# Two-layer adaptive block on one Trainium2 core: layer-0 attention's values and gate turned to have the head dimension on the partitions, with sums of squares as one-column products

## The chip, the core and the metric

The kernel runs on one core of one Trainium2 chip. The metric is device microseconds from launch to end. Three runs of the kernel before gave 1462.98, 1463.49 and 1463.92 us; the median is 1463.49 us. A fourth execution was recorded by the hardware profiler.

The engines are named as in the profile: PE is TensorE's matmul, PEld its weight load, DVE is VectorE, ACT is ScalarE, POOL is GpSimd, SP is SyncE.

## What is computed

The input is 64 sequences of 32 tokens with 256 features, so 2048 tokens. Two layers follow, each with a conditioning step, an attention, a second conditioning step and a feed-forward network. The change touches only layer 0's attention, which for each of 16 heads, with head dimension 128 and 64 slots, computes:

```python
A  = tril(q @ k.T * 128 ** -0.5)          # q, k with rotary embedding
ok = enz * (A @ es)                       # es = exp(s); enz = 1 / cumsum(es)
qv = softmax(ok)
W2 = tril((qv * enz) @ es.T)
o  = W2 @ v                               # v = hs @ Wv.T
g  = hs @ Wg.T
o_n = o * rsqrt(mean(o * o, -1) + 1e-5) * g_norm_weight
out = (o_n * silu(g)) @ Wo.T              # summed over the 16 heads, added to x
```

All arithmetic is float32. Nothing is kept between sequences: the triangle masks are over 32 tokens. In the kernel the softmax's division is left out of `qv`, and the squared sum `rs` goes into the epsilon instead (`e2 = 1e-5 * rs * rs`), since the normalisation that follows removes any factor of a row.

## The kernel before

Layer 0's attention is cut into 32 steps: 4 groups of 4 heads (`hq`) times 8 chunks of 256 tokens (`q`). Each step passes through a dozen stages, and `turn(n)` (line 976) runs stages of four neighbouring steps one after the other, so that each stage's result has time to leave the other engines before the next stage needs it. The order in the source is the order on each engine: nothing is rescheduled, every engine runs its instructions first in, first out. PSUM is one pool of 8 banks; each call of `bank()` takes the bank that was released longest ago, and its first writer waits until the last reader of the bank's former content is done.

A turn's stages in order, with what TensorE does in each (a float32 matmul appears as two matmul records and two weight loads, a transpose as one):

- `slots_exp` (line 748, step n+1): 4 products with 17 rows; ScalarE takes the exponentials.
- `scores` (797, n): 32 products of 64x64 weights and 64 columns; VectorE masks them into `aT`.
- `mix` (878, n-1): 16 products of 64x64 weights and 64 columns, which make W2 transposed; VectorE masks them into `w2T`.
- `leave` (963, n-2): 8 products of 128x128 weights (`ogT`) and 256 columns (`wo`), four accumulated in PSUM for each group of 128 tokens; one VectorE addition of 128x512 puts them on x.
- `project_qk` (693, n+1), first half: 8 products with 256 columns.
- `values` (902, n-1): 16 products, weights `w2T` 64x64, 128 columns of `v`, so that o has tokens on the partitions. The 64x64 weights use a quarter of the array, and the order `quarters` lets four such products run at once. ScalarE then takes 8 times Square of 128x128 with an accumulated sum.
- `attend` (823, n) and `cumsum` (779, n+1): 16 and 8 products on quarters.
- `norm` (927, n-1): VectorE adds `e2`; POOL raises it to the power -0.5, giving `f2` [128 tokens, 8].
- `project_qk`, second half: 8 products with 256 columns.
- `gate` (934, n-1): 8 VectorE instructions of 128x128, o times `f2` (one number for each token) times the gate.
- `weigh` (854, n): POOL multiplies `qv` and `enz` into `qe`; VectorE makes `e2`.
- `project_vg` (725, n), for v and for g: 4 products each with 512 columns (weights are tokens). v is copied by ScalarE; g goes through Silu in 6 instructions of ScalarE.
- `prepare` (199): pieces of the quantisation of later weights, with a few transposes, run at two places of the turn.
- `turn_qe` (867, n): 4 transposes of 128x128, copied by ScalarE.
- `turn_og` (948, n-1): 8 transposes of 128x128, copied by ScalarE in 6 instructions into `ogT`.

After the 32 steps, from about 815 us on, the rest of the kernel works through the same 8 chunks (second conditioning, feed-forward network, layer 1). That part is the same in both kernels. The functions that the change touches, and the turn that calls them:

Of the kernel before, what the change touches and what calls it, by code (L numbers as in the profile page):

```python
# [9 lines left out]
F32 = mybir.dt.float32  # L10
I32 = mybir.dt.int32
AF = mybir.ActivationFunctionType
ALU = mybir.AluOpType
AX = mybir.AxisListType

P = 128
B = 64
T = 32
D = 256
# [56 lines left out]
def mk_kernel(  # L76
# [10 lines left out]
    nc = tc.nc  # L87
    MULT, ADD, SUB, MAX, MIN = ALU.mult, ALU.add, ALU.subtract, ALU.max, ALU.min
# [5 lines left out]
    def bank():  # L94
        return psum.tile([P, 512], F32, tag="ps", name="ps")
# [11 lines left out]
    ident = const("ident")  # L107


    xq = [keep.tile([P, 2, D], F32, tag=f"x{q}", name=f"x{q}") for q in range(8)]  # L110
# [23 lines left out]
    ones = keep.tile([P, P], F32, tag="ones", name="ones")  # L134
    mhalf = keep.tile([P, 8], F32, tag="mhalf", name="mhalf")
# [433 lines left out]
    with ExitStack() as s1:  # L569
        p1 = s1.enter_context(tc.tile_pool(name="p1", bufs=1))  # L570
        work = s1.enter_context(tc.tile_pool(name="work", bufs=2))
# [117 lines left out]
        def at(i):  # L689
            hq, q = steps[i]  # L690
            return hq, q, weights[hq], hsT[q // 2], (q % 2) * 256, state[i]
# [30 lines left out]
        def by_parity(ap):  # L722
            return ap.rearrange("p (r e d) -> p r e d", r=2, e=2)

        def project_vg(i, which):
            hq, q, w, hs, lo, s = at(i)
            wt = w[2 if which == "v" else 3]
            for gi in range(2):
                ps = bank()
                for c in range(2):  # L730
                    nc.tensor.matmul(  # L731
                        ps, lhsT=hs[:, c, lo + gi * P : lo + (gi + 1) * P], rhs=wt[:, c, :],
                        start=(c == 0), stop=(c == 1),
                    )
                t = work.tile([P, 512], F32, tag=which, name=which, bufs=2)
                if which == "v":
                    nc.scalar.copy(t, ps)
                else:
                    to, of = by_parity(t), by_parity(ps)
                    nc.scalar.activation(to[:, :, 0, :], of[:, :, 0, :], AF.Silu)  # L740
                    for half in range(2):
                        here, there = slice(half * 64, half * 64 + 64), slice(64 - half * 64, P - half * 64)
                        nc.scalar.activation(to[here, :, 1, :], of[there, :, 1, :], AF.Silu)
                s[which, gi] = t

        E32 = float(np.exp(np.float32(32.0)))

# [23 lines left out]
        def quarters(product):  # L771


            for e in range(2):
                for at in range(2):
                    out = at ^ e
                    product(e, slice(64 * at, 64 * at + 64), slice(64 * out, 64 * out + 64))
# [76 lines left out]
        def weigh(i):  # L854
            s = state[i]
            qe = work.tile([P, 512], F32, tag="qe", name="qe", bufs=1)
            nc.gpsimd.tensor_tensor(
                qe.rearrange("p (k e m) -> p e k m", k=4, e=2),
                s["qv"].rearrange("p (e k) m -> p e k m", e=2),
                s["enz"].rearrange("p e (k m) -> p e k m", k=4), MULT,  # L860
            )

            e2 = work.tile([P, 8], F32, tag="e2", name="e2")
            nc.vector.scalar_tensor_tensor(e2, s["rs"], 1e-5, s["rs"], MULT, MULT)
            s["qe"], s["e2"] = qe, e2

        def turn_qe(i):
# [32 lines left out]
            s["w2T"] = w2T  # L900

        def values(i):
            s = state[i]
            f = work.tile([P, 8], F32, tag="f", name="f")
            s["f"] = f
            po = [bank(), bank()]
            s["po"] = po
            for k in range(4):
                gi, pr = k // 2, k % 2

                def product(e, rows, out):
                    h = pr * 2 + e
                    nc.tensor.matmul(  # L913
                        po[e][out, k * P : (k + 1) * P], lhsT=s["w2T"][rows, e, k, :],
                        rhs=s["v", gi][rows, h * P : (h + 1) * P], start=True, stop=True,
                    )

                quarters(product)
            for e in range(2):
                for k in range(4):  # L920
                    sq = work.tile([P, P], F32, tag="sq", name="sq", bufs=1)
                    nc.scalar.activation(  # L922
                        sq, po[e][:, k * P : (k + 1) * P], AF.Square,
                        accum_out=f[:, e * 4 + k : e * 4 + k + 1],
                    )

        def norm(i):
            s = state[i]
            nc.vector.scalar_tensor_tensor(s["f"], s["f"], 1.0 / P, s["e2"], MULT, ADD)  # L929
            f2 = work.tile([P, 8], F32, tag="f2", name="f2")  # L930
            nc.gpsimd.tensor_tensor(f2, s["f"], mhalf, ALU.pow)  # L931
            s["f2"] = f2

        def gate(i):

            s = state[i]
            f2 = s["f2"]
            for gi in range(2):
                s["og", gi] = work.tile([P, 4, P], F32, tag="og", name="og")
            for k in range(4):  # L940
                for e in range(2):
                    gi, h = k // 2, k % 2 * 2 + e
                    nc.vector.scalar_tensor_tensor(
                        s["og", gi][:, h, :], s["po"][e][:, k * P : (k + 1) * P],
                        f2[:, e * 4 + k : e * 4 + k + 1], s["g", gi][:, h * P : (h + 1) * P], MULT, MULT,
                    )

        def turn_og(i):
            s = state[i]
            for gi in range(2):  # L950
                ps = bank()
                for h in range(4):
                    nc.tensor.transpose(ps[:, h * P : (h + 1) * P], s["og", gi][:, h, :], ident)  # L953
                t = work.tile([P, 4, P], F32, tag="ogT", name="ogT")
                to = t.rearrange("p (r e) t -> p r e t", e=2)
                of = ps.rearrange("p (r e t) -> p r e t", r=2, e=2)
                nc.scalar.copy(to[:, :, 0, :], of[:, :, 0, :])
                for half in range(2):
                    here, there = slice(half * 64, half * 64 + 64), slice(64 - half * 64, P - half * 64)
                    nc.scalar.copy(to[:, :, 1, here], of[:, :, 1, there])  # L960
                s["ogT", gi] = t

        def leave(i):
            hq, q, w, hs, lo, s = at(i)
            ps = bank()
            for gi in range(2):
                for h in range(4):
                    nc.tensor.matmul(  # L968
                        ps[:, gi * D : (gi + 1) * D], lhsT=s["ogT", gi][:, h, :], rhs=w[4][:, h, :],
                        start=(h == 0), stop=(h == 3),  # L970
                    )
            xf = xq[q].rearrange("p g f -> p (g f)")
            nc.vector.tensor_tensor(xf, ps, xf, ADD)
            s.clear()

        def turn(n):

            def on(i, f, *a):
                if 0 <= i < len(steps):
                    f(i, *a)  # L980

            def more(*at):

                if n in at:
                    next(beyond)

            def ahead():
                if 2 <= n < len(steps):
                    next(preparing, None)

            N = len(steps)
            on(n + 1, slots_exp)
            on(n, scores)
            more(N)
            on(n - 1, mix)
            on(n + 1, slots_clip)
            more(N - 1)
            on(n - 2, leave)
            more(N - 1)
            on(n + 1, project_qk, "q", 0)  # L1000
            on(n + 1, project_qk, "k", 0)
            if n < 2:
                condition(n + 2)
            on(n - 1, values)
            on(n, attend)
            on(n + 1, cumsum)
            more(N)
            on(n - 1, norm)
            on(n + 1, project_qk, "q", 1)
            on(n + 1, project_qk, "k", 1)  # L1010
            on(n - 1, gate)
            on(n, weigh)
            on(n, project_vg, "v")
            on(n, project_vg, "g")
            if n < 2:
                low_rank(n + 2)
            if n < 1:
                gather_cond(n + 3)
            if n == 1:
                small_tables()  # L1020
            ahead()
            more(N - 1)
            on(n, turn_qe)
            on(n - 1, turn_og)
            more(N)
            ahead()

# [559 lines left out]
```

## Time and profile before

| what | us |
|---|---|
| median of three runs | 1463.49 |
| the profiled execution's own time | 1462.34 |
| its span, first to last instruction | 1460.6 |
| matmul busy, whole span | 1411.5 (97%) |
| a turn of layer-0 attention, from one `turn_og` to the next (381.11 to 404.72) | 23.61 |
| in that turn: PE, PEld, DVE, ACT, POOL busy | 23.61, 17.35, 16.57, 14.90, 8.44 |

The granted TensorE clock was 0.988 over the span. A line of the profile's timeline gives the start in us, the duration in us from the first record's start to the last one's end, the engine, the source line, the operation, the tiles written and read, the shape and the number of records. Neighbouring PE lines overlap by the pipeline's depth, so the time that a group takes of the engine is the distance from its start to the start of the next group, not its duration.

### The profile page before, as it was taken

How to read it: one execution, taken by the hardware profiler on the slowest of the kernel's cores; microseconds unless marked ns; L12 is line 12 of the kernel's file. 1: busy time of each engine (PE TensorE's matmuls, PEld its weight loads, DVE VectorE, ACT ScalarE, POOL GpSimd, SP SyncE). 2: the span in 40 equal slices, each digit the busy share in tenths (PEclk: the TensorE clock that was granted, in tenths of full speed). 3: DMA queues.
4: the chain of work that ended last, by engine and by line, in shares of the span. 5: the costliest groups of instructions: out<-in, count | busy, mean ns of one | idle time of the engine just before them, and what ended most of it. 6: DMA issues, size and time to landing. Idle time of an engine off the chain costs nothing.

```text
span 1460.6 us, 37036 instructions
## 1 busy us (share of the span) xinstructions
PE 1411.5 (97%) x15496; PEld 1082.4 (74%) x15496; DVE 827.1 (57%) x1899; ACT 617.0 (42%) x2014; POOL 514.4 (35%) x586
## 2 busy tenths in 40 slices
PE   5899999999999999999999999999999999999997
PEld 3666777777777777667767878788887878787865
DVE  2566677776768676667565224363636263534555
ACT  1355575656566575746566312121312121222121
POOL 3433243333424243324354243333252515152130
PEclk9999999999999999999999999999999999999999
DMA  6201010100111000100001222122221212121120
GB/s 182 55 2 66 2 30 31 34 2 12 33 39 41 9 9 12 46 2 1 13 16 50 72 79 74 52 73 59 58 75 55 78 38 84 41 73 46 43 77 18
DMA packets 61503, 65.14 MB, mean 45 GB/s; under 512 B 34901, under 2 KB 48853, under 8 KB 61337
## 3 DMA queue, kind: packets, MB, share of 16 engines
q0 software_dynamic: 13312, 35.93, 8.8%
q1 hardware_dynamic: 44824, 22.33, 5.6%
q10 hardware_dynamic: 3200, 4.52, 1.0%
q8 instruction: 122, 2.00, 0.6%
q14 instruction: 45, 0.36, 0.1%
HBM read 60.66 MB, written 3.93 MB: 44 GB/s over the span
## 4 chain that ended last, share of the span: by engine, by line
PE 92%; DMA 2%; DVE 2%; issue 2%; ACT 1%; SPq 1%; POOL 0%; DVEq 0%; POOLq 0%; ACTq 0%
PE ps L700 16%; PE ps L731 15%; PE ps L968 8%; PE ps L436 8%; PE ps L507 5%; PE ps L1301 5%; PE ps L482 3%; PE ps L1341 3%; PE ps L1098 3%; PE ps L526 3%; PE ps L913 2%; PE ps L810 2%; PE ps L450 2%; PE ps L953 2%; PE ps L888 1%
## 5 line engine op out<-in xcount | busy, mean ns | idle before, releaser
L714 POOL TENSOR_TENSOR qT<-ra,rb 128x256 f32<-128x256 f32 x64 | 46.5, 727 | 365.0 <-DVE rb L712 365.0
L922 ACT ACTIVATE sq<-ps 128x128 f32<-128x128 f32 x256 | 70.9, 277 | 213.9 <-PE ps L913 206.8
L368 POOL DMA_INDIRECT we<-in_ew,at x64 | 61.4, 960 | 255.5 <-DVE at L366 170.6
L968 PE MATMUL ps<-wo,ogT 128*128 128x256 f32 x512 | 123.3, 396 | 6.7 <-DVE aT L817 6.7
L700 PE MATMUL ps<-hsT,wq 128*128 128x256 f32 x512 | 126.5, 391 | 0.0
L700 PE MATMUL ps<-hsT,wk 128*128 128x256 f32 x512 | 121.5, 380 | 0.0
L711 DVE TENSOR_TENSOR ra<-ps,ct 128x512 f32<-128x512 f32 x128 | 87.6, 684 | 49.1 <-PE ps L700 44.1
L731 PE MATMUL ps<-wv,hsT 128*128 128x512 f32 x256 | 115.2, 593 | 0.0
L731 PE MATMUL ps<-wg,hsT 128*128 128x512 f32 x256 | 115.1, 592 | 0.0
L968 PEld LDWEIGHTS ps<-wo,ogT 128*128 128x128 f32 x512 | 97.8, 196 | 21.9 <-DVE aT L817 7.3
L700 PEld LDWEIGHTS ps<-hsT,wq 128*128 128x128 f32 x512 | 95.6, 192 | 18.3 <-issue 6.0
L794 DVE RECIPROCAL enz<-ps 128x256 f32<-128x256 f32 x64 | 107.5, 1721 | 1.5 <-PE ps L785 1.5
L700 PEld LDWEIGHTS ps<-hsT,wk 128*128 128x128 f32 x512 | 97.9, 191 | 13.4
L931 POOL TENSOR_TENSOR f<-f,mhalf 128x8 f32<-128x8 f32 x32 | 52.9, 1652 | 132.3 <-DVE f L929 132.3
L731 PEld LDWEIGHTS ps<-wg,hsT 128*128 128x128 f32 x256 | 48.7, 190 | 61.2 <-issue 54.0
L712 DVE TENSOR_TENSOR rb<-ps,ct 128x512 f32<-128x512 f32 x128 | 87.2, 681 | 0.0
L848 ACT ACTIVATE qv<-ok,nmx 128x64 f32<-128x64 f32 x256 | 84.9, 335 | 1.9 <-DVE nmx L844 1.9
L731 PEld LDWEIGHTS ps<-wv,hsT 128*128 128x128 f32 x256 | 48.6, 190 | 47.5 <-issue 45.9
L1301 PE MATMUL ps<-guT,y3T 128*128 128x352 f32 x256 | 79.6, 465 | 1.2 <-ACT y3T L347 1.2
L817 DVE SCALAR_TENSOR_TENSOR aT<-ps,ct 128x256 f32<-128x256 f32 x64 | 24.2, 419 | 86.8 <-PE ps L810 86.8
L458 DVE TENSOR_TENSOR hT<-ps,sg 128x256 f32<-128x256 f32 x64 | 24.3, 420 | 83.5 <-ACT sg L457 83.5
L507 PE MATMUL ps<-yT,f 128*128 128x256 f32 x320 | 71.2, 382 | 0.2 <-ACT yT L493 0.2
(225 smaller groups left out, 2985.3 us busy)
## 6 DMA issues: line engine op xcount, KB each, us to landing
x<-in_x SPq DMA_DIRECT2D x8, 256.0 KB, 9.4
wq<-in_wqT SPq DMA_DIRECT2D x16, 128.0 KB, 2.6
wk<-in_wkT SPq DMA_DIRECT2D x16, 128.0 KB, 3.2
wv<-in_wvT SPq DMA_DIRECT2D x4, 512.0 KB, 10.9
wg<-in_wgT SPq DMA_DIRECT2D x4, 512.0 KB, 3.9
wo<-in_woT SPq DMA_DIRECT2D x4, 512.0 KB, 4.7
row<-in_wgu ACTq DMA_DIRECT2D x11, 128.0 KB, 2.7
out<-res SPq DMA_DIRECT2D x5, 256.0 KB, 2.8
```

The lines of the kernel that those rows point to most:

```text
L368: nc.gpsimd.indirect_dma_start(out=to, out_offset=None, in_=table, in_offset=bass.IndirectOffsetOnAxis(ap=at, axis=0))
L436: nc.tensor.matmul(ps[:, i * 256 : (i + 1) * 256], lhsT=mlp[name, k // 4][:, j, part], rhs=c["xT"][:, j, :], start=(i == 0 and j == 0), st ...
L507: nc.tensor.matmul(ps[:, i * 256 : (i + 1) * 256], lhsT=wt[:, j, k * P : (k + 1) * P], rhs=yT[:, j, :], start=(j == 0), stop=(j == 1),)
L700: nc.tensor.matmul(ps[:, half * 256 : (half + 1) * 256], lhsT=wt[:, c, half * 256 + pr * P : half * 256 + (pr + 1) * P], rhs=hs[:, c, lo : ...
L711: nc.vector.tensor_tensor(by_t(a.rearrange("p h t -> p (h t)")), by_t(ps), cosb, MULT)
L712: nc.vector.tensor_tensor(by_t(b.rearrange("p h t -> p (h t)")), by_t(ps), sinb, MULT)
L731: nc.tensor.matmul(ps, lhsT=hs[:, c, lo + gi * P : lo + (gi + 1) * P], rhs=wt[:, c, :], start=(c == 0), stop=(c == 1),)
L794: nc.vector.reciprocal(t[:, e, :], banks[e][:, :256])
L848: nc.scalar.activation(qv[:, k, :], ok[:, k, :], AF.Exp, bias=nmx[:, k : k + 1], accum_out=rs[:, k : k + 1],)
L922: nc.scalar.activation(sq, po[e][:, k * P : (k + 1) * P], AF.Square, accum_out=f[:, e * 4 + k : e * 4 + k + 1],)
L968: nc.tensor.matmul(ps[:, gi * D : (gi + 1) * D], lhsT=s["ogT", gi][:, h, :], rhs=w[4][:, h, :], start=(h == 0), stop=(h == 3),)
L1301: nc.tensor.matmul(ps[:, :352], lhsT=c["y3T"][:, k, gi * P : (gi + 1) * P], rhs=guT[:, k, lo : lo + 352], start=(k == 0), stop=(k == 1),)
```

## The change

Values, gate and the way out change their layout; the numbers computed are the same.

- v is projected as before. The gate is projected with the weights of `wg` stationary and the 256 tokens moving (8 products of 256 columns in place of 4 of 512), so that it has d on the partitions; two Silu instructions of 128x512 take it out of PSUM.
- `values` swaps its operands: v [64 tokens, 128 of d] is stationary, and `w2T` [64 tokens, 64 tokens] moves. o comes out as [128 of d, tokens]. Two products, on the two halves of the rows, can run at once, each writing its own bank. Two Square instructions of 128x512 write the squares to SBUF.
- The sum over d now lies across the partitions: `norm` takes it with 8 products that have the squares [128 of d, 128 tokens] stationary and one column of ones moving.
- `gate` multiplies o and the gate in two VectorE instructions of 128x512 and no longer waits for `norm`. It stands earlier in the turn, and `norm` later, between the projections of v and of the gate.
- `turn_og` and its copies are gone, since og already has d on the partitions.
- `leave` can't accumulate the four heads in PSUM any more, since each head's result [tokens, 256] has to be scaled by its own `f2`. Its 8 products go to four banks, and 8 VectorE instructions of 128x256 multiply by `f2` and add to x.
- `weigh` makes `e2` in three instructions instead of one, since the order of the tokens in half of it changes.

The diff, without the lines in which only names change:

```diff
-        def project_vg(i, which):
+        def project_g(i):
+            g = work.tile([P, 4, 256], F32, tag="g", name="g", bufs=1)
+            for pr in range(2):
+                ps = bank()
+                for e in range(2):
+                    h = pr * 2 + e
+                    for c in range(2):
+                        nc.tensor.matmul(
+                            ps[:, e * 256 : (e + 1) * 256], lhsT=w[3][:, c, h * P : (h + 1) * P],
+                            rhs=hs[:, c, lo : lo + 256], start=(c == 0), stop=(c == 1),
+                        )
+                nc.scalar.activation(
+                    g[:, pr * 2 : pr * 2 + 2, :].rearrange("p e t -> p (e t)"), ps, AF.Silu
+                )
...
         def values(i):
-            for k in range(4):
-                gi, pr = k // 2, k % 2
-                def product(e, rows, out):
-                    h = pr * 2 + e
-                    nc.tensor.matmul(
-                        po[e][out, k * P : (k + 1) * P], lhsT=s["w2T"][rows, e, k, :],
-                        rhs=s["v", gi][rows, h * P : (h + 1) * P], start=True, stop=True,
-                    )
-                quarters(product)
-            for e in range(2):
-                for k in range(4):
-                    sq = work.tile([P, P], F32, tag="sq", name="sq", bufs=1)
-                    nc.scalar.activation(
-                        sq, po[e][:, k * P : (k + 1) * P], AF.Square,
-                        accum_out=f[:, e * 4 + k : e * 4 + k + 1],
-                    )
+            for gi in range(2):
+                for h in range(4):
+                    for half in range(2):
+                        rows = slice(64 * half, 64 * half + 64)
+                        k = gi * 4 + h
+                        nc.tensor.matmul(
+                            po[half][:, k * 64 : (k + 1) * 64], lhsT=s["v", gi][rows, h * P : (h + 1) * P],
+                            rhs=s["w2T"][rows, h % 2, gi * 2 + h // 2, :], start=True, stop=True,
+                        )
+            sq = work.tile([P, 8, 2, 64], F32, tag="sq", name="sq", bufs=1)
+            for half in range(2):
+                nc.scalar.activation(
+                    sq[:, :, half, :], po[half].rearrange("p (k t) -> p k t", k=8), AF.Square
+                )
 
         def norm(i):
-            nc.vector.scalar_tensor_tensor(s["f"], s["f"], 1.0 / P, s["e2"], MULT, ADD)
+            ps = bank()
+            for gi in range(2):
+                for h in range(4):
+                    to = h % 2 * 4 + gi * 2 + h // 2
+                    nc.tensor.matmul(
+                        ps[:, to : to + 1],
+                        lhsT=s["sq"][:, gi * 4 + h, :, :].rearrange("p a t -> p (a t)"), rhs=ones[:, :1],
+                        start=True, stop=True,
+                    )
+            nc.vector.scalar_tensor_tensor(f, ps[:, :8], 1.0 / P, s["e2"], MULT, ADD)
             nc.gpsimd.tensor_tensor(f2, f, mhalf, ALU.pow)
 
         def gate(i):
-            for k in range(4):
-                for e in range(2):
-                    gi, h = k // 2, k % 2 * 2 + e
-                    nc.vector.scalar_tensor_tensor(
-                        s["og", gi][:, h, :], s["po"][e][:, k * P : (k + 1) * P],
-                        f2[:, e * 4 + k : e * 4 + k + 1], s["g", gi][:, h * P : (h + 1) * P], MULT, MULT,
-                    )
+            for half in range(2):
+                nc.vector.tensor_tensor(
+                    to[:, half], s["po"][half].rearrange("p (g h t) -> p g h t", g=2, h=4), by[:, half], MULT
+                )
 
-        def turn_og(i):
-                    nc.tensor.transpose(ps[:, h * P : (h + 1) * P], s["og", gi][:, h, :], ident)
...
         def leave(i):
-            ps = bank()
             for gi in range(2):
-                for h in range(4):
-                    nc.tensor.matmul(
-                        ps[:, gi * D : (gi + 1) * D], lhsT=s["ogT", gi][:, h, :], rhs=w[4][:, h, :],
-                        start=(h == 0), stop=(h == 3),
-                    )
-            nc.vector.tensor_tensor(xf, ps, xf, ADD)
+                for pr in range(2):
+                    ps = bank()
+                    for e in range(2):
+                        h = pr * 2 + e
+                        nc.tensor.matmul(
+                            ps[:, e * D : (e + 1) * D], lhsT=s["og"][:, h, gi * P : (gi + 1) * P],
+                            rhs=w[4][:, h, :], start=True, stop=True,
+                        )
+                    for e in range(2):
+                        of = e * 4 + gi * 2 + pr
+                        nc.vector.scalar_tensor_tensor(
+                            xq[q][:, gi, :], ps[:, e * D : (e + 1) * D], s["f2"][:, of : of + 1],
+                            xq[q][:, gi, :], MULT, ADD,
+                        )
 
         def turn(n):
-            on(n - 1, norm)
+            on(n - 1, gate)
             on(n + 1, project_qk, "q", 1)
             on(n + 1, project_qk, "k", 1)
-            on(n - 1, gate)
             on(n, weigh)
-            on(n, project_vg, "v")
-            on(n, project_vg, "g")
+            on(n, project_v)
+            on(n - 1, norm)
+            on(n, project_g)
...
             on(n, turn_qe)
-            on(n - 1, turn_og)
```

## The prediction, made blind

> **What bounds the kernel now.** I read the first part of the page (busy time), then the slices, then the order in time of one engine, and only then the groups.
>
> ```profile
> PE 1411.5 (97%) x15496; PEld 1082.4 (74%) x15496; DVE 827.1 (57%) x1899; ACT 617.0 (42%) x2014; POOL 514.4 (35%) x586
> PE   5899999999999999999999999999999999999997
> PEclk9999999999999999999999999999999999999999
> ```
>
> TensorE is busy throughout at an undisturbed clock; nothing else passes 57%. So work taken off the other engines is worth nothing by itself, and I need TensorE's time by stage. This is one turn of layer-0 attention in the timeline of TensorE:
>
> ```profile
> 381.11 1.04 PE L953 MATMUL ps<-ct,og 128*128 128x128 f32 x8
> ...
> 383.70 0.97 PE L888 MATMUL ps<-qeT,es 64*64 64x64 f32 x32
> 384.60 3.72 PE L968 MATMUL ps<-wo,ogT 128*128 128x256 f32 x16
> 388.16 1.89 PE L700 MATMUL ps<-hsT,wq 128*128 128x256 f32 x8
> 389.88 1.89 PE L700 MATMUL ps<-hsT,wk 128*128 128x256 f32 x8
> 391.70 1.10 PE L913 MATMUL ps<-v,w2T 64*64 64x128 f32 x32
> 392.63 0.64 PE L831 MATMUL ps<-es,aT 64*64 64x64 f32 x32
> ...
> 397.20 3.60 PE L731 MATMUL ps<-wv,hsT 128*128 128x512 f32 x8
> 400.63 3.60 PE L731 MATMUL ps<-wg,hsT 128*128 128x512 f32 x8
> 404.07 0.38 PE L249 MATMUL ps<-ct,row 128*128 128x128 f32 x2
> 404.29 0.60 PE L871 MATMUL ps<-ct,qe 128*128 128x128 f32 x4
> 404.72 1.04 PE L953 MATMUL ps<-ct,og 128*128 128x128 f32 x8
> ```
>
> From start to start: transposes of og (L953) 0.97, mix (L888) 0.90, leave 3.56, values (L913) 0.93, gate (second L731) 3.44 us. Each group begins where the former ends, and a turn is 23.61 us. In it DVE has 16.57 us of work and ACT 14.90. So 32 turns lengthen or shorten by what TensorE gains or loses, as long as no new wait arises.
>
> **The limit that a busy row hides** is the weight load. Every product has one, and it is free only while the product before it streams long enough. Two places show one not covered. The first is the adapters' product, with weights of 128 columns in 32 rows and only 64 moving columns, on four row groups at once:
>
> ```profile
> 812.83 2.02 PE L450 MATMUL ps<-u,bx 32*128 32x64 f32 x64
> 814.77 0.69 PE L888 MATMUL ps<-qeT,es 64*64 64x64 f32 x32
> 815.40 0.92 PE L968 MATMUL ps<-wo,ogT 128*128 128x256 f32 x3
> ```
>
> 64 records are 16 rounds of four; 1.94 us / 16 = 0.121, and less some 0.15 us for leaving this tiling, 0.112 us a round. The stream alone would be about half: 512 columns take 0.429 us (3.44 / 8), so 64 take 0.054. The second is a product with one moving column:
>
> ```profile
> L222 PEld LDWEIGHTS ps<-part,ones x6: 190/190/191, 145.5 to 286.0; 128*128 128x128 f32 x6
> L222 PE MATMUL ps<-part,ones x6: 167/208/250, 146.0 to 286.1; 128*128 128x1 f32 x6
> ```
>
> The columns are least, median and most. Of the two records of such a product, which start 28 ns apart in the trace, the first takes 167 ns and the second 250: it ends 28 + 83 = 111 ns later, held by its own load.
>
> **What the Trainium skill says.** "TensorE: Matmul & The Clock Gate", section "LDWEIGHTS (loading the stationary operand)": a load takes its columns divided by 1.2 GHz, whatever the rows; for 128 columns that is 107 ns. The trace agrees (0.112 and 0.111 us). "TensorEngine Tiling (Array Packing)", section "Instruction Overhead": "Don't take tiling factor from a dimension that's already small". The 64 columns of `w2T` are that; the L450 rows agree. The same page, "Key Properties": changing the tiling mode drains the engine; the trace has 0.97 for eight transposes of 0.109, so 0.1 us for the change to L762's rows.
>
> **The change, part by part** (per turn, TensorE).
>
> 1. Gate projection. Removed: 8 records of 512 columns, 3.44. Added: 16 of 256; L700 does 8 in 1.72, so 3.44. Its loads hide as L700's do. Zero; without that cover 16 x 0.112 = 1.79 would still be less than the stream.
> 2. Values. Removed 0.93 (four 64x64 products at once, 128 columns). Added: 32 records on two row groups, 16 rounds, weights of 128 columns, 64 moving. By L450 a round is 0.112: 1.79, plus 0.05 to 0.15 for the change from 64x128 to 64x64 tiling; I take 0.10. 1.89 - 0.93 = +0.96. Bounds: +0.02 if a round costs its stream only (16 x 0.054 + 0.10 = 0.96, and 0.93 is gone); +2.75 if the two row groups' loads don't overlap (32 x 0.112 + 0.10).
> 3. One-column products: 16 records, each with a load of 128 columns and nothing to stream: 16 x 0.111 = +1.78. Bounds: 16 x 0.028 = 0.45 if only the record spacing counted; 16 x 0.112 = 1.79 plus a drain of 0.1.
> 4. Transposes of og: -8 x 0.109 = -0.87. The 0.1 us for changing the tiling stays, after L871.
> 5. Leave: 16 records of 256 columns as before; accumulating or not, no difference: 0.
> 6. Mix. Its second bank waits now for the last copy of `ogT`: that copy is the 383.43 one of ScalarE's timeline and ends at 383.94; in the chain of waits the last 28 records begin at 383.99. The same 32 records at 814.77, with the copies long done, take 0.63. So this turn loses 0.27. From the starts of all turns, the loss is near 0.27 in 13 of them, 0.21 in 10, 0.07 in 4, none at the end: 3.5 + 2.1 + 0.3 = 5.9 us in all. After the change mix waits only for the copy of `qeT` (ended 382.70 against 383.70): gone. Next in line there is scores' end, which is TensorE itself.
> 7. Near 620 us mix and leave together lose some 6 us, because VectorE sits on the load of a row of `in_wdown` (6.37 us) before it can mask. That landing doesn't move, and TensorE arrives about 1.1 us earlier (0.87 + 0.27): +1 us once.
>
> Sum: 32 x (0.96 + 1.78 - 0.87) = 59.8; 59.8 - 5.9 + 1.0 = +54.9 us.
>
> **Waits that the change adds**, and their cover. Behind the one-column products, in TensorE's order, stand the gate's projection and all the rest; they wait for the two Square instructions, which can start when values ends. A 128x512 copy on ScalarE (L737) takes 0.585; two are 1.2 us. Between values and them lie attend, cumsum, half of project_qk and v: 392.63 to 400.63, 8.0 us. Covered by 6.8; if the cover went, 1.2.
> Gate (two VectorE instructions of 128x512, 0.68 each as L711) now stands ahead of the rotary products, which end at about 401.7 instead of 400.4 in the clock of the turn above; POOL then needs about 1.7 more for the last two sums and 1.27 for `qe`: 404.6. `turn_qe` follows 1.78 later than now, at 405.9. Cover 1.2 us.
> POOL's power (1.65 us) moves behind `qe`; its reader, the way out, is some 4 us later in the next turn.
> Leave's 8 VectorE instructions: L817 (128x256 out of PSUM) takes 0.42; 8 are 3.4 us at most, and cumsum's second bank waits for the eighth. That one can't end before leave's end plus 0.5; cumsum comes 5.9 us after leave (half of project_qk 3.5, values 1.9, attend 0.5). Leave's four banks wait for `aT` and `w2T`, the last ready at 385.4; the fourth is wanted at 384.60 + 2.67 = 387.3. VectorE grows by 8 x 0.38 + 2 x 0.68 + 0.2 - 2.15 - 0.69 = 1.8 us to about 18.4 of 25.5: no bound. ScalarE loses squares, Silu pieces and copies; off the path, worth nothing beyond point 6.
>
> **The sum against the times.** The profiled execution took 1462.34 us with a span of 1460.6; 1462.34 + 54.9 = 1517.2. It lies 1.15 below the median 1463.49, so as a median: 1518.4. I say 1518.
>
> **Rivals.**
> - *Uncovered loads are not paid* (the end on the other side). If TensorE took the next weights in ahead, values would cost +0.02 and the one-column products 0.45: per turn 0.02 + 0.45 - 0.87 = -0.40, x 32 = -12.8, with points 6 and 7 -17.7: 1446. With one exposed load costing t, a turn changes by 32t + 0.10 - 0.93 - 0.87 and about 0.15 for points 6 and 7: the sign turns at t = 0.058 us. For it: loads are pulled ahead everywhere in this trace. Against: 0.111 and 0.112 in two places.
> - *Values alone are cheap*: L450's round may be long for its pattern (two runs of 32 columns), not its load: 54.9 - 30.1 = +25: 1488.
> - *One-column products alone are cheap*: 54.9 - 42.6 = +12: 1476. Against: L222's 83 ns.
> - *Two row groups load one after the other*: another 57 us, 1576. Against: L450's four groups in 0.112.
> - *A new wait*: `qe` on POOL has the thinnest cover, 1.2 us, and the shift of VectorE's work could eat it: 0.3 to 1 us a turn, +10 to +30: 1528 to 1548.
> The instructions of the changed kernel stand in the order that the diff says, so that it does nothing of the sort is no case.
>
> **Chances.** Likeliest 0.68 (1518, its own range 1508 to 1530: the 0.1 of tiling either way is 3 us, a load of 0.107 to 0.115 another 4, points 6 and 7 about 5). New wait 0.10, values cheap 0.06, one column cheap 0.05, loads not paid 0.06, serial groups 0.05. Range: 1485 to 1540 leaves out one column cheap, loads not paid, serial groups, and the ends of the likeliest and of the new wait: near 0.2. Faster by over 0.2% (about what a measurement of this kernel can tell from no change) 0.06, within 0.01, slower 0.93.
>
> **What would show it.** In the timeline after: values' 32 records about 1.9 us from start to start; the one-column group about 1.8; mix 0.63; a turn about 25.3 to 25.5 us, still with no gap on TensorE. If values take under 1.2 or the one-column products under 1.0, the load was hidden and steps 2 or 3 are wrong; if TensorE shows gaps before `turn_qe`, cumsum or scores, the covers are.

## The result, and the profile after

| | before | after |
|---|---|---|
| median, us | 1463.34 (1462.98 to 1463.92, 4 runs) | 1532.71 (1531.14 to 1534.1, 4 runs) |
| profiled execution, us (span) | 1462.34 (1460.6) | 1531.78 (1530.0) |
| one turn in mid-phase, us | 23.61 | 25.40 |

The changed kernel is slower: the ratio is 1.0473, with a 95% interval of 1.0455 to 1.0492. The profiled execution is 69.4 us longer; the sum had +54.9. The first two parts of the page after, to be set beside the three lines of before:

```profile
PE 1470.9 (96%) x16008; PEld 1187.9 (78%) x16008; DVE 944.2 (62%) x1995; ACT 484.2 (32%) x1246; POOL 516.1 (34%) x586
...
PE   5898999999999999989999999999999999999987
...
PEclk9999999999999999999999999999999999999999
```

TensorE is still full at an undisturbed clock, with 512 records more. ScalarE lost 133 us of work and it bought nothing; VectorE gained 117. One turn in TensorE's timeline (start, busy time, count at the end):

```profile
404.12 1.84 PE L947 MATMUL ps<-ones,sq 128*128 128x1 f32 x16
405.82 3.70 PE L747 MATMUL ps<-hsT,wg 128*128 128x256 f32 x16
409.36 0.38 PE L249 MATMUL ps<-ct,row 128*128 128x128 f32 x2
409.57 0.60 PE L887 MATMUL ps<-ct,qe 128*128 128x128 f32 x4
...
411.73 0.65 PE L904 MATMUL ps<-qeT,es 64*64 64x64 f32 x32
412.42 3.72 PE L978 MATMUL ps<-wo,og 128*128 128x256 f32 x16
...
419.53 2.00 PE L929 MATMUL ps<-w2T,v 64*128 64x64 f32 x32
421.46 0.69 PE L841 MATMUL ps<-es,aT 64*64 64x64 f32 x32
421.97 0.62 PE L795 MATMUL ps<-es,ct 64*64 64x128 f32 x16
...
429.51 1.84 PE L947 MATMUL ps<-ones,sq 128*128 128x1 f32 x16
```

Read from start to start: the one-column group 1.70 us, the gate 3.54, leave 3.56, the values 1.93 (0.92 before), attend 0.51 (0.46), mix 0.69 (0.90). From one L947 to the next is 25.39 us, again without a gap. In a group of L947 every record after the first takes 250 ns and starts 0.112 us after the one before it, as the second record of the L222 product did on which the prediction was built:

```profile
L947 PEld LDWEIGHTS ps<-ones,sq x512: 190/192/193, 90.2 to 892.0; 128*128 128x128 f32 x171
L947 PE MATMUL ps<-ones,sq x512: 167/250/251, 90.6 to 892.1; 128*128 128x1 f32 x171
```

(The three numbers behind `x512` are the least, median and most of a record's duration, in ns.)

### The profile page after: what moved, and what is told of

It reads as the page before. It is cut to its first block, busy times and chain, and to the rows that moved or that the text cites. A ratio compares the mean times of both kernels' runs of the same rounds, so it can differ in the third digit from the quotient of the medians.

```text
span 1530.0 us, 37314 instructions
## 1 busy us (share of the span) xinstructions
PE 1470.9 (96%) x16008; PEld 1187.9 (78%) x16008; DVE 944.2 (62%) x1995; ACT 484.2 (32%) x1246; POOL 516.1 (34%) x586
## 4 chain that ended last, share of the span: by engine, by line
PE 92%; DVE 3%; DMA 2%; issue 1%; ACT 1%; SPq 0%; POOL 0%; DVEq 0%; ACTq 0%
PE ps L700 15%; PE ps L978 8%; PE ps L747 7%; PE ps L436 7%; PE ps L730 7%; PE ps L507 5%; PE ps L1314 5%; PE ps L929 4%; PE ps L482 4%; PE ps L947 4%; PE ps L1354 3%; PE ps L1111 3%; PE ps L526 3%; PE ps L820 2%; PE ps L450 2%
## 5 line engine op out<-in xcount | busy, mean ns | idle before, releaser
L978 PE MATMUL ps<-wo,og 128*128 128x256 f32 x512 | 123.6, 396 | 8.4 <-DVE aT L827 7.0
L984 DVE SCALAR_TENSOR_TENSOR x<-ps,f,x 128x256 f32<-128x256 f32 x256 | 120.9, 482 | 15.4 <-PE ps L978 3.2
L747 PE MATMUL ps<-hsT,wg 128*128 128x256 f32 x512 | 118.3, 384 | 0.0
L978 PEld LDWEIGHTS ps<-wo,og 128*128 128x128 f32 x512 | 97.9, 196 | 25.4 <-DVE aT L827 12.0
L935 ACT ACTIVATE sq<-ps 128x512 f32<-128x512 f32 x64 | 34.7, 595 | 252.6 <-PE ps L929 252.6
L747 PEld LDWEIGHTS ps<-hsT,wg 128*128 128x128 f32 x512 | 94.9, 190 | 12.0 <-issue 0.5
L947 PEld LDWEIGHTS ps<-ones,sq 128*128 128x128 f32 x512 | 62.2, 192 | 14.9 <-issue 14.8
```

The source lines that it names most:

```text
L747: nc.tensor.matmul(ps[:, e * 256 : (e + 1) * 256], lhsT=w[3][:, c, h * P : (h + 1) * P], rhs=hs[:, c, lo : lo + 256], start=(c == 0), stop ...
L947: nc.tensor.matmul(ps[:, to : to + 1], lhsT=s["sq"][:, gi * 4 + h, :, :].rearrange("p a t -> p (a t)"), rhs=ones[:, :1], start=True, stop= ...
L978: nc.tensor.matmul(ps[:, e * D : (e + 1) * D], lhsT=s["og"][:, h, gi * P : (gi + 1) * P], rhs=w[4][:, h, :], start=True, stop=True,)
L984: nc.vector.scalar_tensor_tensor(xq[q][:, gi, :], ps[:, e * D : (e + 1) * D], s["f2"][:, of : of + 1], xq[q][:, gi, :], MULT, ADD,)
```

## The experiments

My theory: the added time is the exposed weight loads of the values and of the one-column products, and the rest is stalls in which VectorE stands behind a transfer. Its rivals: some fixed cost per product; the shape of the values' operands; and VectorE's added work. All twelve kernels ran on two chips on which the kernel before takes some 1551 us, since TensorE's granted clock falls to half in many short stretches, mostly after 670 us. So I compare ratios to the kernel before, and regular turns between 140 and 670 us. There the clock is whole in most runs, but for a stretch at the stall of the 25th turn, and a few more in e3 and e8. The expectations in us were written for the time of 1463 us. The changed kernel itself wasn't run there; its turns of 25.18 (25.40 with the transposes of prepare) come back unchanged in e2 and e7, whose ratios of 1.0443 and 1.0449 stand for it.

### e1: the one-column products left out

```diff
-                    nc.tensor.matmul(ps[:, to : to + 1], lhsT=s["sq"]..., rhs=ones[:, :1], start=True, stop=True)
-            nc.vector.scalar_tensor_tensor(f, ps[:, :8], 1.0 / P, s["e2"], MULT, ADD)
+            nc.vector.scalar_tensor_tensor(f, s["sq"][:, 0, 0, :8], 1.0 / P, s["e2"], MULT, ADD)
```

> The changed kernel without the 8 one-column products of each step: the sum of squares is left out, and f is made from eight of the squares, so the output's scale is not the reference's. Theory (every exposed load of 128 columns costs 0.11 us): the group takes 1.70 us of a turn and leaves the first load of the gate's projection exposed for 0.10 more, so 32 x 1.80 = 58 us less, near 1475 us. Rival (the loss over the forecast comes from new waits around the products, on the squares or on the power): a turn shortens by more than these 1.80 us, since the waits go too, or by less, because another wait takes their place; then the time is below 1465 or above 1485.

Measured: ratio 1.0164 (1.0141 to 1.0187), a turn of 23.98 instead of 25.40. That is 1.42 less, not 1.80 (and 1.20 less in the turns that took 25.18). So the rival's second case holds: another wait takes part of the products' place. The timelines of TensorE and of GpSimd in this kernel show what took the place of the rest:

```profile
417.00 0.38 PE L249 MATMUL ps<-ct,row 128*128 128x128 f32 x2
417.53 0.66 PE L887 MATMUL ps<-ct,qe 128*128 128x128 f32 x4
```

```profile
416.20 1.27 POOL L867 TENSOR_TENSOR qe<-qv,enz 128x512 f32<-128x512 f32 x1
```

L887 begins 0.53 us after L249 where 0.21 is its length, right after `qe` ends (416.20 + 1.27 = 417.47). The products cost 1.80, and 0.38 of that would be spent on waiting for `qe` without them. In the changed kernel `qe` ended at 408.06, 1.5 us ahead of its reader at 409.57: the prediction had given it 1.2 us.

### e2: sixty-four columns instead of one

```diff
-                        ps[:, to : to + 1], ... rhs=ones[:, :1],
+                        ps[:, to * 64 : (to + 1) * 64], ... rhs=ones[:, :64],
```

`f` then reads the first of each 64 columns.

> The changed kernel with 64 columns of ones in place of one in each of the 8 products, same result. Theory (the load is the cost, the stream hides under it): no change, 1530 to 1536 us. Rival (the cost is in what streams, or in a fixed price of each product to which the stream adds): 63 columns at 0.84 ns are 53 ns for each of 16 records, 32 x 0.85 = 27 us more, near 1560.

Measured: ratio 1.0443 (1.042 to 1.0467); the group 1.730 us against 1.703, every turn as in the changed kernel. Sixty-four times the stream costs 0.03 us for the whole group. So the price of such a product is not its stream; that it is the load, and not a fixed price of each product, is left to e4.

### e3: the values' loads doubled

```diff
+                        for t0 in (0, 32):
-                            po[half][:, k * 64 : (k + 1) * 64], ... rhs=s["w2T"][rows, h % 2, gi * 2 + h // 2, :]
+                                po[half][:, k * 64 + t0 : k * 64 + t0 + 32], ... rhs=s["w2T"][..., t0 : t0 + 32]
```

> The changed kernel with each product of the values cut into two of 32 moving columns, so that the same columns stream but twice as many weights of 128 columns are loaded. Theory: 16 rounds more at 0.112 us, 32 x 1.79 = 57 us more, near 1590. Rival (a round lasts as long as its columns and its drain): the same columns, no change beyond 5 us.

Measured: the values 3.71 us instead of 1.93, a turn of 26.96 (27.18), 1.78 more; ratio 1.0978 (1.0952 to 1.1003). 64 records on two row groups are 32 rounds of 0.116. The same columns stream; the loads are twice as many, and so is the time.

### e4: the one-column products in four column groups

```diff
+                    for c in range(4):
+                        cols = slice(32 * c, 32 * c + 32)
-                        ps[:, to : to + 1], lhsT=s["sq"]..., rhs=ones[:, :1],
+                            ps[cols, to : to + 1], lhsT=s["sq"]...[:, cols], rhs=ones[:, :1],
```

> The changed kernel with each one-column product cut into four of 32 weights, on the four column groups of the array, same result. Theory (the load's length is its columns, and the loads of different column groups run together): 16 rounds of about 0.03 us and two changes of tiling of 0.1, so 0.7 us instead of 1.80, 32 x 1.1 = 35 us less, near 1497. Rival (each product has a floor, whatever its load): four times as many products, no gain or up to 30 us more.

Measured: a turn of 24.23 (24.45), 0.95 less; ratio 1.0276 (1.0252 to 1.03). TensorE's timeline:

```profile
397.71 0.71 PE L949 MATMUL ps<-ones,sq 128*32 128x1 f32 x64
398.35 3.72 PE L747 MATMUL ps<-hsT,wg 128*128 128x256 f32 x16
```

Four times the products take 0.64 us where 1.70 was; 0.11 comes back in the groups before and behind it, at the changes of tiling. A fixed price per product is out. The Trainium skill, "TensorE: Matmul & The Clock Gate", section "LDWEIGHTS (loading the stationary operand)", has a load take its columns divided by 1.2 GHz; for 32 columns I estimate 27 ns from that. A round of four records is 0.64 / 16 = 0.040 us here, so it shortens nearly as the page says, and the 0.013 above it are not explained.

### e5: the values on four quadrants

```diff
+                        for dh in range(2):
-                            po[half][:, k * 64 : (k + 1) * 64], lhsT=s["v", gi][rows, h * P : (h + 1) * P],
+                                po[half][64 * dh : 64 * dh + 64, k * 64 : (k + 1) * 64],
+                                lhsT=s["v", gi][rows, h * P + 64 * dh : h * P + 64 * dh + 64],
```

> The changed kernel with each 64x128 block of values cut in two 64x64 weights, so that the values come as 64 products on the four quadrants of the array (half of the contraction by half of d), as the kernel before has them, with the same result. Theory (the values cost a whole turn's worth of weight loads, which two row groups can hide less well than four quadrants): the group from the first product of values to attend goes from 1.93 us back to about 0.93 us, the turn of 25.18 or 25.40 us to about 24.1 or 24.35, the ratio to the kernel before from 1.045 to about 1.024. Rival (transposed values are slow for what they read, columns of v as weights, not for the shape of the loads): within 0.2 us of 1.93 and a ratio of 1.045.

Measured: the values 0.98 us, attend 0.47, a turn of 24.18 (24.40), 1.00 less; ratio 1.0284 (1.0259 to 1.031). The theory gets its time. The rival (columns of `v` as weights are slow in themselves) is out, since the same columns are the weights here: it was the 128 columns to load for 64 to stream, on only two row groups.

### e6: both tilings

The edits of e4 and e5 together.

> The changed kernel with the values on four quadrants and the one-column products in four column groups of 32 weights, with the same result. If the loads are all that the change costs: 1.03 us less at the values and 0.95 us less at the one-column products in each turn, so a turn of 23.2 us (23.4 with the prepare transposes) where the changed kernel has 25.18 (25.40), which is the turn of the kernel before within 0.2 us; ratio 1.000 to 1.006, the rest being the stalled turns and the last stage. Rival (a wait takes the place of the loads, as the wait for qe of 0.38 us did when the one-column products were left out altogether): a turn of 23.6 us or more and a ratio above 1.012.

Measured: a turn of 23.23 (23.45), ratio 1.0072 (1.0054 to 1.009). A regular turn costs what it cost before (23.19 to 23.61): with the loads shortened, what the change still adds and what it saves on transposes and mix cancel. No wait replaced the loads. Of the 11 us that are left, 4.8 sit in three stalled turns: the 4th, 13th and 25th take 30.63, 25.19 and 31.98 us, against 28.12, 24.34 and 30.56 in the kernel before. The rest I can't place, since the kernel before left no trace on this chip.

### e7: one VectorE instruction on the way out instead of eight

```diff
-                        nc.vector.scalar_tensor_tensor(xq[q][:, gi, :], ps[:, e * D : (e + 1) * D],
-                            s["f2"][:, of : of + 1], xq[q][:, gi, :], MULT, ADD)
+            nc.vector.scalar_tensor_tensor(xf, ps, s["f2"][:, 0:1], xf, MULT, ADD)
```

> The changed kernel with the way out of the four heads accumulated in one bank and added by one VectorE instruction that scales by a single column of f2; it leaves out that each head has a scale of its own, and computes something else. TensorE runs the same products. VectorE has some 3.4 us less to do in a turn (one instruction of about 0.7 us in place of eight of 0.48). Theory (VectorE's work is beside TensorE's in a steady turn, and shows only where VectorE is already stuck behind a transfer): steady turns the same within 0.05 us, the five turns with stalls shorter by 2 to 4 us in all, ratio lower by 0.001 to 0.003 than the changed kernel's 1.045 on such a chip. Rival (VectorE paces part of every turn): 0.2 us or more less in each turn, ratio 1.040 or less.

Measured: ratio 1.0449 (1.043 to 1.0468), every regular turn the same. The three stalled turns take 32.45, 26.99 and 33.83, the same as in the changed kernel (32.52, 27.13, 33.68). VectorE's amount of work is beside the path, as expected; but taking 3.4 us of it away doesn't shorten the stalled turns either, where I had given it 2 to 4 us. That part of the theory fell.

### e8: the kernel before, with copies of `ogT` on VectorE

```diff
-                    nc.scalar.copy(to[:, :, 1, here], of[:, :, 1, there])
+                    nc.vector.tensor_copy(to[:, :, 1, here], of[:, :, 1, there])
```

> The kernel before with the swapped copies of ogT (two of each group's three) on VectorE in place of ScalarE, with the same result. Theory (the wait at mix in the kernel before is for the last copies on ScalarE's queue, and costs 0.21 to 0.27 us in most turns): the wait goes, about 5 us in all, ratio 0.9965; another wait (the decay's product aT on the same VectorE) may take 1 to 2 us of it back. Rival (the copies only change place in the queue, and VectorE's own work is later for them): ratio 1.000 or above.

Measured: slower, ratio 1.0195 (1.0177 to 1.0214); a turn of 25.10 instead of 23.61. The rival holds: I had looked at VectorE's idle time and not at what stands in its queue. VectorE's timeline in this kernel:

```profile
402.16 0.88 DVE L960 COPY ogT<-ps 128x128 f32<-128x128 f32 x4 [4.02 <-ACT ogT L957]
402.96 0.41 DVE L189 TENSOR_REDUCE qs<-row 128x1 f32<-128x256 f32 x1
...
404.51 0.35 DVE L197 TENSOR_SCALAR row<-row,qs 128x256 f32<-128x256 f32 x1
404.78 0.74 DVE L817 SCALAR_TENSOR_TENSOR aT<-ps,ct 128x256 f32<-128x256 f32 x2
```

VectorE stands 4.02 us at these copies, behind ScalarE's. Prepare's six steps, which used to run in just that time, now stand behind them (402.96 to 404.78), and `aT` behind those. The way out, L968, waits for the bank that `aT` reads, 1.37 us in this turn, so that it begins 2.39 us after mix instead of 0.90.

### e9 and e10: prepare's transfers further ahead

In both kernels VectorE's queue has prepare's first reduction in front of `aT`. VectorE's timeline of the changed kernel, in the 4th turn:

```profile
120.25 0.17 DVE L953 SCALAR_TENSOR_TENSOR f<-ps,e 128x8 f32<-128x8 f32 x1
127.63 1.75 DVE L219 TENSOR_REDUCE part<-f 128x1 f32<-128x1536 f32 x1 [7.22 <-DMA f<-in_f1T]
129.30 0.74 DVE L827 SCALAR_TENSOR_TENSOR aT<-ps,ct 128x256 f32<-128x256 f32 x2
```

```diff
         (in prepare, after the loads of f1, f3 and f2w)
+        load_row(0)
+        load_row(1)
+        yield
+        yield
         for t in (f1, f3, f2w):
...
-        load_row(0)
-        load_row(1)
...
                 load_row(k + 2 if k < 10 else k + 1)
+            if k == 11:
+                yield
+                yield
```

> The changed kernel with prepare's transfers further ahead of the VectorE steps that read them: the first two rows are loaded with f1, f3 and f2w, two more turn halves pass before the first reduction, and two before the last row's; same result. In the changed kernel VectorE stands 7.22, 3.18 and 7.44 us behind these transfers in three turns (32.52, 27.13 and 33.68 us long), with aT, on which TensorE waits, queued behind it. Theory: these three turns fall to about 25.4 us, 17 us less in all, ratio about 0.011 below the 1.045 of such a chip, so 1.033 to 1.036; other turns unchanged. Rival (the transfers aren't what holds VectorE there, and aT is late anyway): under 5 us gained, ratio 1.042 or more.

> The kernel before with the same edit of prepare, same result. The same three turns take 28.12 (with its short first group), 24.34 and 30.56 us there, against 23.3 to 23.6 around them. Theory: about 12 us less, ratio 0.992, which is less than the edit gives the changed kernel, since the changed kernel's TensorE reaches these waits earlier after the transfers are issued; this difference, 4 to 6 us, is the part of the change's cost that my sum put at 1 us. Rival (the stalls cost both kernels the same): the same number of us in both within 2.

Measured: e9 has a ratio of 1.0384 (1.0352 to 1.0416), e10 of 0.9924 (0.9895 to 0.9954). The same place in e9:

```profile
123.87 0.17 DVE L957 SCALAR_TENSOR_TENSOR f<-ps,e 128x8 f32<-128x8 f32 x1
128.73 0.76 DVE L831 SCALAR_TENSOR_TENSOR aT<-ps,ct 128x256 f32<-128x256 f32 x2 [4.69 <-PE ps L824]
```

VectorE now waits for TensorE, as it should, and no longer for a transfer. The three turns fall from 93.33 us (32.52 + 27.13 + 33.68) to 77.88 (26.86 + 25.18 + 25.84) in e9, by 15.4, and from 83.02 to 74.00 (26.61 + 23.34 + 24.05) in e10, by 9.0. So the transfers hold VectorE, and in these turns the edit is worth 6.4 us more to the changed kernel. The whole times don't show that. e10 gains the 0.0076 on the kernel before that was expected; e9 gains 0.0065 on the 1.0449 that e7 had on the other chip, which is short of the 0.011 expected, and each has an interval of some 0.003 on either side. By them the rival, the same number of us in both, is not excluded.

There is more in such a stall than the wait. In the kernel before, TensorE's clock stands at half for 3.4 us from 125.3 and for 6.8 us from 623.6, both right at the stalls of the 4th and the 25th turn; in the changed kernel it does so for 6.8 us from 127.9 and from 670.7. In e9, whose longest wait there is 1.56 us, the clock is whole from 112 to 140 and from 640 to 700 us. In e10 3.4 us at half are left in the 4th turn, which is 1.7 of the 6.4 us. Whether the wait brings the clock down is not shown: in e8 ten waits of 1.38 us did not.

### e11 and e12: both tilings and the transfers ahead

e11 is e6 with the edit of e9. e12 also makes `e2` on ScalarE:

```diff
-            nc.vector.scalar_tensor_tensor(e2[:, :4], rs[:, :4], 1e-5, rs[:, :4], MULT, MULT)
+            nc.scalar.activation(e2[:, :4], rs[:, :4], AF.Square, scale=float(np.sqrt(1e-5)))
```

and the two half pieces likewise.

> The changed kernel with the values on four quadrants, the one-column products on four column groups, and prepare's transfers ahead; same result. From the 1.0072 of the two tilings alone, less the stalls in three turns (30.63, 25.19 and 31.98 us, against 23.2 to 23.5 around them, 17 us in all, 0.011): ratio 0.996, between 0.993 and 1.000, so below the kernel before and level with or a little above the kernel before with the same edit of prepare. Rival (a new wait, for qe or aT, comes up once the stalls are gone): above 1.002.

> The same as the last, with the three small products for e2 (0.48 us and two of 0.67 us on VectorE) made as squares on ScalarE; same result. Theory (VectorE's load is beside the path once it stands behind no transfer): turns the same within 0.05 us and a ratio within 0.002 of the last kernel's. Rival (VectorE's 1.8 us of small products push aT back): 0.2 us or more less per turn, ratio lower by 0.004 or more.

Measured: e11 0.9978 (0.9964 to 0.9992), e12 1.0003 (0.9988 to 1.0017). e11 is below both kernels, but e10, the kernel before with the same edit, is lower still (0.9924). In regular turns the two are level (23.23 to 23.45 in e11, 23.19 to 23.62 in e10). The whole attention, from the first scores to `L482`, takes 807.8 us in e11's trace and 801.5 in e10's, and the clock stands at half in it for 30.7 and 20.5 us, which would be some 5 of these 6 us. So this layout of the attention, with its loads repaired, comes level with the old one in its turns and no further. e12's ratio is 0.0025 above e11's, hardly beyond the noise; its turns miss clearly what I expected, on the slow side: three of them take 23.95 us where e11 has 23.24. GpSimd's timeline in one of them, and VectorE's beside it:

```profile
188.98 0.73 POOL L719 TENSOR_TENSOR qT<-ra,rb 128x256 f32<-128x256 f32 x1
189.66 1.05 POOL L718 TENSOR_TENSOR kT<-ra,rb 128x256 f32<-128x256 f32 x1
190.66 1.04 POOL L719 TENSOR_TENSOR kT<-ra,rb 128x256 f32<-128x256 f32 x1
191.67 1.58 POOL L871 TENSOR_TENSOR qe<-qv,enz 128x512 f32<-128x512 f32 x1
```

```profile
189.30 0.82 DVE L236 TENSOR_SCALAR f<-f,tsc 128x768 f32<-128x768 f32 x1
190.04 1.08 DVE L233 TENSOR_SCALAR f<-f,trc 128x768 f32<-128x768 f32 x1
191.16 0.97 DVE L234 TENSOR_SCALAR f<-f 128x768 f32<-128x768 f32 x1
```

Without the small products VectorE reaches prepare's large steps 1.8 us sooner, while GpSimd still makes `kT` and `qe`. Both grow (`kT` 1.05 for 0.73, L233 1.08 for 0.61 in e11), and `qe`, whose cover the shorter turn has nearly used up, comes late: TensorE waits for it, three times for 0.5 us, and the turn is 0.7 us longer. In e11 GpSimd is the first to start: `kT` and `qe` keep their 0.73 and 1.26 us, and it is VectorE's L236 that takes 1.52.

## Why the prediction was right in its mechanism and short in its size

By its own steps; the difference to explain is 69.4 - 54.9 = 14.5 us. The sums are over all steps, from start to start in TensorE's two timelines.

- **Step 1 (gate projection at zero)**: 3.54 instead of 3.44. The first load after the one-column products is not covered, 0.10; counted below.
- **Step 2 (values, +0.96)**: 0.92 to 1.93, +1.01, and attend behind them +0.05, which goes again when both use the same tiling (e5). That is 33.7 us instead of 30.7: right in kind (e3, e5), short by 3.0, and within the bounds that were given (the lower one should read +0.03, from 0.96 - 0.93).
- **Step 3 (one-column products, +1.78)**: 1.70 for the group and 0.10 for the gate's first load. That is 57.8 us instead of 57.0, short by 0.8 (e2 and e4 show that it is the load).
- **Step 4 (transposes, -0.87)**: the group of 0.97 is gone and 0.09 went to L887 (0.44 to 0.53), as written: 28.0 us instead of 27.8, which takes 0.2 off the difference.
- **Step 5 (leave at zero)**: 3.56 before and after, for TensorE. VectorE's share was mis-sized: its eight instructions take 0.48 each, not 0.38 to 0.42, with no effect (e7).
- **Step 6 (mix, -5.9 us in all)**: mix goes to 0.69, not 0.63. The claim that TensorE itself is next in line failed. In the turn shown mix's last record started at 412.16, the first half of `aT` on VectorE was ready at 412.37, and leave began at 412.42: `aT` was the next to be late. Outside the three stalled turns the gain is 0.21 in 11 turns, 0.145 in 6 and 0.5 in one; in the 28th to 31st mix takes 0.89 to 0.92, which loses 0.07 in each and stays unexplained. In all 3.4 us. Short by 2.5.
- **Step 7 (stall near 620 us, +1)**: miscounted. I followed one transfer, and there are three, which the waits of the kernel before would have shown. TensorE's waits for `aT` (total us, times, longest), first the kernel before, then the changed one:

```profile
PE ps L968 <- DVE aT L817: 6.7, 3, 3.5
```

```profile
PE ps L978 <- DVE aT L827: 7.0, 2, 5.2
PE ps L904 <- DVE aT L827: 3.7, 1, 3.7
```

They grow by 1.21, 1.06 and 1.75 us in the 4th, 13th and 25th turn, the first two by about the 1.1 that was meant for one. Beyond what every turn gains (2.0), the three turns grew by 2.4, 0.8 and 1.1 us, 4.3 in all instead of 1. Short by 3.3.
- **Not in the sum at all: what follows the attention.** From the first scores to `L482` the shift is 64.3 us, and the parts above make 33.7 + 57.8 - 28.0 - 3.4 + 4.3 = 64.4. From there to the end 5.1 more are lost, 3.5 of them in one place near the end. The rows give the busy times of the engines, then granted clock, DMA share and GB/s, for two stretches of 6.8 us of the kernel before and for the same work in the changed one:

```profile
1414.50:1421.30 6.80, 4.20 (x136) 3.13 (x135) 5.26 (x10) 1.40 (x5) 0.06 (x1) 0.82 0.11 36
1421.30:1428.10 6.80, 5.27 (x30) 4.06 (x32) 2.75 (x6) 0.59 (x1) 0.00 (x0) 0.92 0.06 19
```

```profile
1486.40:1493.20 6.80, 5.94 (x28) 4.70 (x29) 1.15 (x5) 1.14 (x4) 0.00 (x0) 0.50 0.01 2
```

L1354's products take 5.28 us where 3.98 was, and the group ahead of them, L1221, takes 3.80 instead of 1.64, with a gap of 2.07 us that no event of the profile explains. The kernel before has half the clock here too, but for 3.4 us and not 6.8. Over all that follows the attention both traces stand at half for about the same time, 10.9 and 10.2 us, so the clock alone doesn't make the 5.1. Nothing in the change touches this work, and on the chips of e1 to e12 nothing of the kind is seen: from `L482` to the end it is 694.8 and 696.5 us in the two kernels with the old layout and 694.3 to 697.1 in the ten with the new one. So the 5.1 us belong to this pair of traces or to their chip, and their cause stays open.

The parts add up: 3.0 + 0.8 - 0.2 + 2.5 + 3.3 + 5.1 = 14.5. All but one go the same way, so no error was hidden by another.

The measured 1532.7 lies outside the 1508 to 1530 of the likeliest path and inside the 1528 to 1548 of the rival "a new wait". By the time alone that rival would have been taken; the timeline decides against it, since TensorE's groups follow without a gap and `qe` ends 1.5 us ahead of its reader.

The other rivals: "loads not paid", "values cheap" and "one column cheap" fell with the 1.93 and 1.70 us of the two groups (e3, e2 and e4 show the load behind them), and "serial groups" with the 1.93. The wait for `qe` came as soon as the products were gone (e1) or GpSimd was slowed (e12). As for what I had said would show: values about 1.9, products about 1.8 with the gate's first load, a turn of 25.3 to 25.5 without gaps were seen; mix at 0.63 was not.

## What to carry to other kernels

Before turning a product round, count its loads: a weight of 128 columns that streams only a few columns costs its load, 0.11 us per record here, however little it computes, and cutting the weights into column groups (e4, e5) recovers most of it. An engine with idle time is not free: ask what is queued behind the instruction that you put there (e8), and with whom it will run at the same time (e12). When a step waits for a transfer in an engine's queue, issuing the transfer a turn earlier (e10) can be worth more than the rearrangement in question.

## What the hardware showed that I had not expected

The three small products for `e2`, of four columns each, take 0.48 and two times 0.67 us in the changed kernel, where one of eight columns took 0.16 before. VectorE's timeline, and GpSimd's:

```profile
404.99 0.48 DVE L875 SCALAR_TENSOR_TENSOR e<-rs 128x4 f32<-128x4 f32 x1
405.49 1.35 DVE L878 SCALAR_TENSOR_TENSOR e<-rs 64x4 f32<-64x4 f32 x2
```

```profile
405.41 0.73 POOL L714 TENSOR_TENSOR kT<-ra,rb 128x256 f32<-128x256 f32 x1
406.10 0.73 POOL L715 TENSOR_TENSOR kT<-ra,rb 128x256 f32<-128x256 f32 x1
406.78 1.28 POOL L867 TENSOR_TENSOR qe<-qv,enz 128x512 f32<-128x512 f32 x1
```

The first ends at 405.47 and the last at 406.84, each 0.06 us after a GpSimd instruction gives way to the next (405.41, 406.78). The Trainium skill, "SBUF — State Buffer", section "Who interferes with whom", says that a VectorE instruction with two inputs in SBUF contends with a GpSimd instruction that reads SBUF, and that the second to come is blocked until the first ends. The trace agrees, and the last step of the changed kernel shows it. There GpSimd is free until `qe` begins at 864.53:

```profile
863.10 0.16 DVE L875 SCALAR_TENSOR_TENSOR e<-rs 128x4 f32<-128x4 f32 x1 [1.64 <-ACT qv L858]
864.42 1.39 DVE L878 SCALAR_TENSOR_TENSOR e<-rs 64x4 f32<-64x4 f32 x2 [1.16 <-ACT qv L858]
```

```profile
864.53 1.26 POOL L867 TENSOR_TENSOR qe<-qv,enz 128x512 f32<-128x512 f32 x1 [9.61 <-issue]
```

The first product, alone, takes 0.16 us instead of 0.48. Of the two of L878 the first starts ahead of `qe` and takes 0.16; the second starts behind it, takes 1.22 instead of 0.67, and ends 0.02 us after `qe`. So these small instructions measure GpSimd's work, not their own. In e12, too, VectorE's large steps and GpSimd's products grew while they ran side by side; but those steps read one tensor, which is not the case quoted here.
